# The DRAM copy of the transposed adjacency as 8-bit floats, loaded from GpSimd's queue

## The chip, the cores and the metric

The kernel runs on one core of a Trainium2 chip. The metric is the device time of one execution in microseconds. Three runs of the kernel before gave 2100.93, 2103.20 and 2105.14 us; the median is 2103.2 us. One more execution was profiled.

In the profile the engines are called PE (TensorE, matrix products), PEld (TensorE's weight loads, which overlap PE), DVE (VectorE), ACT (ScalarE), POOL (GpSimd) and SP (SyncE, which here only issues transfers). "SPq" and "POOLq" are the queues from which SP and POOL issue DMAs.

## What is computed

Two graph layers over N = 4096 nodes with 512 features. The adjacency matrix holds only zeros and ones, and is symmetric with a full diagonal. Cut to what matters (H = 8 heads, FH = 64 features a head):

```
# layer 0: graph attention with dense scores
feats   = einsum('nf,hfo->hno', x, W)
s_self  = einsum('hno,ho->hn', feats, a_self)
s_neigh = einsum('hno,ho->hn', feats, a_neigh)
dense   = s_self[:, :, None] + s_neigh[:, None, :]
dense   = where(dense > 0, dense, 0.2 * dense) * adj[None]
out     = einsum('hij,hjo->hio', softmax(dense, -1), feats) + b
x       = layernorm(x + relu(concat_heads(out)))
# layer 1: attention inside 32 graphs of 128 nodes
q, k, v = x @ Wq.T + bq, x @ Wk.T + bk, x @ Wv.T + bv
a       = where(same_graph, q @ k.T / sqrt(512), 0)
scores  = (a + adj + adj) * where(same_graph, 1, -1e6)
x       = layernorm(x + (softmax(scores, -1) * same_graph) @ v)
```

Note that a node without an edge still takes part in the softmax of layer 0, with score 0.

## The kernel before

The program holds two ways through the computation. `general_path` (line 33) is taken only for inputs that the fast one can't serve, and a flag that is computed on the chip skips it here. All the time lies in `adjacency_streamed_path` (line 405).

**Setup (to about 170 us).** Features, scores and their exponentials are computed for all nodes and put into DRAM (`g_d`, `f_d`, `pu_d`).

**Four passes, `main_pass(r)` (line 1263), two heads each.** A pass runs over 4 chunks `c` of C = 1024 target nodes, and in a chunk over 32 tiles `j` of 128 source nodes. For each (c, j) it needs `at`, a tile of A transposed: 128 source nodes in the partitions, 1024 target nodes along the row, in fp32 (512 KB). Three engines read `at`:

- VectorE makes `q` from it for each of the two heads (line 1310): the larger of `p_row` and a number of each source node, times `at`.
- ScalarE, and for one in eight VectorE, turns `q` into `mark` (lines 1319 and 1315).
- TensorE multiplies features with `at` into `accf` (line 1330), with `q` into `acc` (line 1347), and weights with `mark` into `dens` (line 1361). In pass 0 it also reads the upper half of each `at` element as bf16 (line 1374).

Work goes in cycles of `wide` tiles: 8 in passes 0 to 2, 4 in pass 3.

**Where `at` comes from: `bring` (line 1074).** In pass 0 (r = 0) GpSimd's queue loads four tiles' worth of the adjacency at once and converts it from fp32 to fp8 (`load_adjacency`, line 569, tile `a_b`); TensorE transposes it two columns at a time (line 1088), ScalarE copies the result as fp32 into `at` (line 1092), and GpSimd's queue stores it into `at_d` in DRAM (line 1093). In passes 1 to 3, `at` is loaded again from `at_d` (line 1078), by SP's queue: 3 x 128 = 384 loads. `at` has a ring of 12 buffers in passes 0 to 2 (`MORE` = 6 are added to 6) and of 6 in pass 3, so a load waits until `q`, `accf` and, in pass 0, the store have done with the tile 12 or 6 before.

**Other work on the two queues.** SP issues the loads of `f_s` and `g_s` (lines 1291 and 1295), of `p_row` and `u_row` at the start of a chunk (1269 and 1272), of `ck` (1101: the adjacency in small parts, which ScalarE checks for values other than zero and one), and in pass 3 of layer 1's inputs `x1b`, `hp_l` and `a4` (1116, 1118, 942) and the last outputs (1053). GpSimd issues, after pass 0, only the stores `hs_d` at the end of a chunk (1212) and the outputs (1053), and does small arithmetic on a few columns in pass 3: the powers of the layer norms (527 and 528) and the offsets, minima and sums of layer 1's softmax (974 to 976, 1003 to 1006, 1019 and 1020).

**Pass 3** is interleaved with layer 1: the generator `layer_1` (line 931) is advanced in pieces between the matrix products, after each chunk's rows are finished by `sums_to_rows` (line 1127) and `rows_of_layer_0` (line 1112).

**What sets the order.** The order of TensorE's instructions is that of the program text (line 455). The order on every other engine and queue is chosen at build time by a scheduler from the expected times of the instructions; each engine and queue then runs strictly in that order, and an instruction that waits holds up all that stand behind it. Waits and buffers are derived from the tiles.

Of the kernel before, what the change touches and what calls it, by code (L numbers as in the profile page):

```python
# [10 lines left out]
F32 = mybir.dt.float32  # L11
# [8 lines left out]
P = 128  # L20
# [384 lines left out]
def adjacency_streamed_path(  # L405
# [29 lines left out]
    nc = tc.nc  # L435
    N, F = x.shape
    H, _, FH = W.shape
    NT = N // P
# [5 lines left out]
    FP8 = mybir.dt.float8e4  # L444
    C = 1024
    CT = C // P
    NCH = N // C
# [12 lines left out]
    dram = ctx.enter_context(tc.tile_pool(name="fdram", bufs=1, space=DRAM))  # L460
# [1 line left out]
    g_d = dram.tile([PR, NT // 4, P, 4 * FP], F32, name="g_d")  # L462
    f_d = dram.tile([PR, NT // 4, P, 4 * 2 * FP], F32, name="f_d")
    pu_d = dram.tile([2 * H, N], F32, name="pu_d")
    at_d = dram.tile([NCH, NT, P, C], F32, name="at_d")
    hs_d = dram.tile([N, FP * (PR - 1)], F32, name="hs_d")

    ident = const.tile([P, P], F32, name="ident_f")
# [79 lines left out]
    def misc(shape, dtype=F32):  # L548

        banks.append(banks.pop(0))  # L550
        return banks[-1].tile(shape, dtype, name="ps_m")
# [4 lines left out]
    def ring(name, pool, n):  # L556

        if name not in more:
            return pool
        k = turns[name] % (n + more[name][1])  # L560
        turns[name] += 1
        return pool if k < n else more[name][0]
# [6 lines left out]
    def load_adjacency(c, j):  # L569

        a_b = pools["adj"].tile([P, CT, 4 * P], FP8, name="a_b8")
        a_bs[c, j] = a_b
        return nc.gpsimd.dma_start(
            a_b, adj[ts(c, C), j * P : (j + 4) * P].rearrange("(t p) n -> p t n", p=P)
        )


    with tc.tile_pool(name="setup1", bufs=1, side="right") as one, tc.tile_pool(
        name="setup2", bufs=2, side="right"
    ) as two, tc.tile_pool(name="setup3", bufs=3, side="right") as three, tc.tile_pool(  # L580
        name="xtp", bufs=4, side="right"
# [492 lines left out]
    def bring(r, c, j):  # L1074

        if r:
            at = ats[r, c, j] = ring("at", atp, 6).tile([P, C], F32R, name="at")
            nc.sync.dma_start(at.bitcast(F32), at_d[c, j])
            return
        if j % 2:  # L1080
            return
        if j % 4 == 0 and (c, j) not in a_bs:
            load_adjacency(c, j)
        pairs = a_bs[c, j - j % 4].rearrange("p t n -> p (t n)").bitcast(BF16)
        pairs = pairs.rearrange("p (t k n) -> p t k n", t=CT, k=2)[:, :, j % 4 // 2, :]
        pt = misc([P, CT, P], BF16)
        for t in range(CT):
            nc.tensor.transpose(pt[:, t, :], pairs[:, t, :], ident_b)
        both = pt.rearrange("p t n -> p (t n)").bitcast(FP8).rearrange("p (n k) -> p n k", k=2)
        for k in range(2):  # L1090
            at = ats[r, c, j + k] = ring("at", atp, 6).tile([P, C], F32R, name="at")
            nc.scalar.copy(at, both[:, :, k])  # L1092
            nc.gpsimd.dma_start(at_d[c, j + k], at.bitcast(F32))  # L1093
# [169 lines left out]
    def main_pass(r, ae=None, wide=4):  # L1263

        for c in range(NCH):
# [19 lines left out]
            for j0 in range(0, NT, wide):  # L1285
# [10 lines left out]
                if at_step == 0:  # L1296
                    for j in cycle:
                        bring(0, 0, j)
# [39 lines left out]
                for x_ in follow[:first]:  # L1338
                    bring(*x_)
# [41 lines left out]
                for x_ in follow[first:]:  # L1381
                    bring(*x_)
# [37 lines left out]
    with tc.tile_pool(name="lp", bufs=2) as lp, tc.tile_pool(  # L1420
        name="lp1", bufs=1
# [7 lines left out]
@with_exitstack  # L1429
def tile_gat_then_graph_attention(ctx: ExitStack, tc: tile.TileContext, *args: bass.AP):  # L1430
    nc = tc.nc
    keep = ctx.enter_context(tc.tile_pool(name="flag", bufs=1))
    flag = keep.tile([1, 1], I32, name="flag")
    adjacency_streamed_path(tc, flag, *args)
    other = nc.values_load(flag[0:1, 0:1], min_val=0, max_val=1)
    with tc.If(other > 0):
        general_path(tc, *args)
# [42 lines left out]
```

## Time and profile before

| What | Value |
|---|---|
| Runs, median | 2103.2 us (2100.93 to 2105.14) |
| Profiled execution, its own time | 2104.88 us |
| its span, first to last instruction | 2102.9 us |
| granted TensorE clock | 0.992 |
| bytes moved by DMA | 551.28 MB, mean 262 GB/s |
| HBM read and written | 491.79 MB and 107.22 MB |
| GpSimd busy | 249.4 us, 391 instructions |
| Stores `at_d`, first and last issue | 174.1 and 584.1 us |
| Loads `at`, first and last issue | 577.4 and 1941.9 us |

The span is the time between the first and the last instruction of the profiled execution; some 2 us lie around it. "Idle" of an engine is split by what ended it: an arrow `X <- Y` says that X waited and Y released it. The durations of matrix products are those of a pipeline, so a busy TensorE need not be at its peak. The DMA share is the mean busy share of 16 DMA engines; it can pass 1 where packets of two queues overlap. Bytes of a converting transfer are counted as they are written. Pass 0 runs from about 170 to 604 us, passes 1 and 2 to about 1391, pass 3 with layer 1 to about 1990, and the rest of layer 1 to the end.

### The profile page before, as it was taken

To read this page: it belongs to the slowest core of one execution; us is meant where nothing else is said; L and a number is where in the kernel's file an instruction comes from. 1 tells how busy PE (TensorE), PEld (TensorE's weight loads), DVE (VectorE), ACT (ScalarE), POOL (GpSimd) and SP (SyncE) were. 2 spreads that over 40 slices of the span, in tenths; PEclk is the share of its full clock that TensorE was granted. 3 is DMA by queue.
4 is the path that set the end of the run, shared out by engine and by line. 5 is a ranking of instruction groups with operands and counts; after the bars stand their busy time and mean duration, and the time that the engine had idled before them with its cause. 6 is when DMAs were issued, how large, how long until landed. Compare 5 with 4: busy or idle time off the path is not lost. (4 is left out here: it accounts for less than half of the span.)

```text
span 2102.9 us, 38131 instructions
## 1 busy us (share of the span) xinstructions
PE 2061.3 (98%) x15012; PEld 1015.0 (48%) x15012; DVE 1659.0 (79%) x2032; ACT 1535.7 (73%) x1818; POOL 249.4 (12%) x391
## 2 busy tenths in 40 slices
PE   8999999999999999999999999999999999999997
PEld 4545555454445544445444544444454444445443
DVE  5547788878788998787999989999975884886654
ACT  3327998888868889787899989998876666567420
POOL 2333222222100000000000000000300210210110
PEclk9999999999999999999999999999999999999999
DMA  8999999999889999887999999989964674675211
GB/s 246 270 211 243 287 285 271 294 263 278 263 286 327 338 361 344 297 301 239 323 324 343 311 327 337 334 281 362 305 238 152 239 243 144 225 270 163 73 48 42
DMA packets 207881, 551.28 MB, mean 262 GB/s; under 512 B 25292, under 2 KB 66252, under 8 KB 207692
## 3 DMA queue, kind: packets, MB, share of 16 engines
q1 hardware_dynamic: 140748, 425.79, 58.3%
q0 software_dynamic: 62784, 121.91, 23.3%
q8 instruction: 120, 1.97, 0.4%
q10 hardware_dynamic: 4160, 1.05, 0.2%
q14 instruction: 69, 0.57, 0.1%
HBM read 491.79 MB, written 107.22 MB: 285 GB/s over the span
## 5 line engine op out<-in xcount | busy, mean ns | idle before, releaser
L1310 DVE SCALAR_TENSOR_TENSOR q<-p_row,d_all,at 128x1024 f32<-128x1024 f32 x1024 | 1242.5, 1277 | 180.2 <-PE acc L1347 146.2
L1319 ACT ACTIVATE mark<-q,nb_all 128x1024 fp8e4<-128x1024 f32 x896 | 994.6, 1145 | 192.1 <-DVE q L1310 176.7
L1347 PE MATMUL acc<-q,g_s 128*32 128x512 f32 x8192 | 907.3, 594 | 3.3 <-DVE q L1310 2.9
L1347 PEld LDWEIGHTS acc<-q,g_s 128*32 128x32 f32 x8192 | 265.1, 110 | 599.2 <-issue 532.9
L1330 PE MATMUL accf<-at,f_s 128*128 128x512 f32 x2048 | 494.4, 397 | 5.5 <-DMA at<-at_d 3.9
L1330 PEld LDWEIGHTS accf<-at,f_s 128*128 128x128 f32 x2048 | 378.7, 188 | 116.0 <-issue 25.6
L1107 ACT ACTIVATE ck<-ck,neg_half_f 128x1024 f32<-128x1024 f32 x128 | 145.9, 1140 | 22.1 <-DMA ck<-in_adj_dram 22.1
L1108 ACT ACTIVATE ck<-ck,neg_quarter 128x1024 f32<-128x1024 f32 x128 | 146.3, 1143 | 1.8
L1092 ACT CAST at<-ps_m 128x1024 fp32r<-128x1024 fp8e4 x128 | 120.1, 1026 | 10.4 <-issue 5.9
L1361 PE MATMUL dens<-mark,e_b 128*6 128x512 fp8e4 x2048 | 125.0, 379 | 1.2 <-ACT mark L1319 1.2
L715 PE MATMUL ps_set<-w_sb_f,xT_f 128*128 128x512 f32 x256 | 116.4, 603 | 0.0
L957 PE MATMUL ps_m<-x1T,M_sb 128*128 128x512 f32 x256 | 113.1, 595 | 1.2 <-ACT x1T L938 1.2
L1029 PE MATMUL ps_m<-wvT,x1T 128*128 128x512 f32 x256 | 114.2, 594 | 0.0
L1212 POOL DMA_DIRECT2D hs_d<-hst x12 | 10.7, 895 | 849.6 <-DVE hst L1202 755.6
L1315 DVE TENSOR_SCALAR mark<-q,d_all 128x1024 fp8e4<-128x1024 f32 x128 | 95.7, 748 | 4.8
L737 ACT ACTIVATE fst<-fb 128x512 fp32r<-128x512 f32 x32 | 20.3, 633 | 101.5 <-DMA f_d<-fst 76.8
L1361 PEld LDWEIGHTS <-e_b 128*6 128x6 bf16 x2048 | 52.7, 86 | 81.0 <-issue 37.2
L1093 POOL DMA_DIRECT2D at_d<-at x128 | 68.7, 537 | 181.3 <-ACT at L1092 104.0
L957 PEld LDWEIGHTS ps_m<-x1T,M_sb 128*128 128x128 f32 x256 | 47.9, 190 | 62.7 <-issue 60.1
L1029 PEld LDWEIGHTS ps_m<-wvT,x1T 128*128 128x128 f32 x256 | 47.6, 190 | 57.2 <-issue 56.0
L715 PEld LDWEIGHTS ps_set<-w_sb_f,xT_f 128*128 128x128 f32 x256 | 49.1, 199 | 49.7 <-issue 49.4
L1037 DVE TENSOR_TENSOR v_t<-ps_m,bv_row 128x512 f32<-128x512 f32 x32 | 21.9, 684 | 62.2 <-PE ps_m L1029 62.2
(172 smaller groups left out, 1141.6 us busy)
## 6 DMA issues: line engine op xcount, KB each, us to landing
at<-at_d SPq DMA_DIRECT2D x384, 512.0 KB, 6.1
ck<-in_adj_dram SPq DMA_DIRECT2D x128, 512.0 KB, 5.4
f_s<-f_d SPq DMA_DIRECT2D x128, 512.0 KB, 7.6
at_d<-at POOLq DMA_DIRECT2D x128, 512.0 KB, 15.2
g_s<-g_d SPq DMA_DIRECT2D x128, 256.0 KB, 5.7
f_d<-fst POOLq DMA_DIRECT2D x32, 512.0 KB, 6.3
p_row<-pu_d SPq DMA_DIRECT2D x32, 512.0 KB, 7.1
a_b<-in_adj_dram POOLq DMA_DIRECT2D x32, 512.0 KB, 17.2
```

The costliest lines, as they stand in the source:

```text
L715: nc.tensor.matmul(pf, tile_j(xTs[k][:, c].rearrange("p u n -> p (u n)"), u), w_sb[:, c, :], start=(c == 0), stop=(c == FC - 1),)
L957: nc.tensor.matmul(pz, L1["M"][:, f, ts(c, P)], x1T[:, f, :], start=(f == 0), stop=(f == FC - 1),)
L1029: nc.tensor.matmul(pv, x1T[:, f, ts(u, P)], L1["wvT"][:, f, :], start=(f == 0), stop=(f == FC - 1),)
L1092: nc.scalar.copy(at, both[:, :, k])
L1107: tc.keep_in_program_order(nc.scalar.activation(ck, ck, AF.Square, bias=neg_half))
L1108: nc.scalar.activation(ck, ck, AF.Abs, bias=neg_quarter, accum_out=binp[:, k : k + 1])
L1310: nc.vector.scalar_tensor_tensor(q, p_row[h], d_j, ats[r, c, j].bitcast(F32), op0=OP.max, op1=OP.mult)
L1315: nc.vector.tensor_scalar(mark, q, d_j, None, op0=OP.is_gt, saturate=False)
L1319: nc.scalar.activation(mark, q, AF.Sigmoid, bias=nb_all[:, j, hh : hh + 1], scale=BIG, saturate=False,)
L1330: nc.tensor.matmul(accf[:, s, :], f_s[j // 4][:, j % 4, w, :], ats[r, c, j][:, ts(s, HB)], start=(j == 0 and w == 0), stop=(j == NT - 1 an ...
L1347: nc.tensor.matmul(acc[o : o + 32, s, :], g_s[j // 4][:, j % 4, h, o % FH : o % FH + 32], qs[j, h][:, ts(s, HB)], start=(j == 0), stop=(j ...
L1361: nc.tensor.matmul(dens[lo : lo + 6, :], e_b[:, j, 2 * r + h, :], marks[j, h][:, ts(s, HB)], start=(j == 0), stop=(j == NT - 1),)
```

## The change

```diff
@@ adjacency_streamed_path @@
-    at_d = dram.tile([NCH, NT, P, C], F32, name="at_d")
+    at_d = dram.tile([NCH, NT, P, C], FP8, name="at_d")
@@ bring @@
         if r:
             at = ats[r, c, j] = ring("at", atp, 6).tile([P, C], F32R, name="at")
-            nc.sync.dma_start(at.bitcast(F32), at_d[c, j])
+            nc.gpsimd.dma_start(at.bitcast(F32), at_d[c, j])
             return
```

The copy in DRAM holds a byte per element instead of four: 128 KB a tile, 16.8 MB in all instead of 67.1 MB. Zeros and ones are exact in it. The store of line 1093 is unchanged in the text, but now converts fp32 to fp8 on its way. The load of line 1078 converts fp8 to fp32 and is issued by GpSimd's queue instead of SP's. Tiles in SBUF, rings, cycles and all computing instructions stay as they are in the text; the scheduler places the moved loads anew.

## The prediction, made before the result was known

> **What bounds the kernel now.** I read the page's busy shares first, then the busy time by stretches, then who waited for whom, then the DMA part, and last the order of time on GpSimd's queue, because that is the queue the loads move to.
>
> ```profile
> PE 2061.3 (98%) x15012; PEld 1015.0 (48%) x15012; DVE 1659.0 (79%) x2032; ACT 1535.7 (73%) x1818; POOL 249.4 (12%) x391
> ```
>
> TensorE works 98% of the span. The stretches show where the other 42 us are (columns: engine, busy us; then clock, DMA share, GB/s):
>
> ```profile
> 260.00:700.00 440.00, 433.53 (x3888) 217.72 (x3890) 362.10 (x365) 367.66 (x362) 75.63 (x125) 1.00 1.01 283
> 700.00:1140.00 440.00, 438.95 (x3516) 214.89 (x3507) 385.06 (x367) 376.19 (x403) 3.54 (x4) 0.99 0.91 319
> 1140.00:1600.00 460.00, 456.94 (x3615) 217.27 (x3614) 410.07 (x434) 402.55 (x455) 26.16 (x21) 1.00 0.86 305
> ...
> 600.00:1000.00 400.00, 393.87 (x3134) 194.30 (x3136) 342.60 (x342) 329.63 (x352) 4.69 (x6) 0.99 0.89 313
> 1000.00:1400.00 400.00, 400.00 (x3348) 189.76 (x3344) 373.39 (x354) 359.74 (x376) 3.54 (x4) 1.00 0.92 321
> ...
> 1980.00:2103.00 123.00, 106.62 (x378) 54.59 (x370) 60.11 (x164) 21.43 (x58) 17.11 (x43) 0.97 0.17 60
> ```
>
> From 260 to 1600, where the copy is written and mostly read, TensorE idles 6.5 + 1.0 + 3.1 = 10.6 us. The rest is the setup (14 us before 260) and the tail (16 us after 1980), which hold none of the changed transfers. So even perfect loads cannot give more than about 11 us. TensorE's direct wait for the copy is smaller still (us in total, times, longest):
>
> ```profile
> PE accf L1330 <- DMA at<-at_d: 3.9, 2, 2.9
> ...
> PEld accf L1330 <- DMA at<-at_d: 7.5, 7, 3.3
> ...
> SPq L1078 <- DVE q L1310: 359.9, 192, 9.5
> ...
> POOL off L974 <- ACT a L967: 31.7, 7, 11.7
> ```
>
> Both 3.9 us waits are at the first cycle of pass 1 (608 to 616). The third line says that the loads themselves wait on SP's queue until the VectorE has released a buffer: 192 times, 1.9 us on average. The DMA part:
>
> ```profile
> at<-at_d SPq DMA_DIRECT2D x384, 512.0 KB, 6.1
> ...
> at_d<-at POOLq DMA_DIRECT2D x128, 512.0 KB, 15.2
> ...
> a_b<-in_adj_dram POOLq DMA_DIRECT2D x32, 512.0 KB, 17.2
> ```
>
> The DMA engines are 89 to 92% taken in passes 1 and 2, but nothing on TensorE's path waits for them after 616.
>
> **What the Trainium skill says.** "DMA: Bandwidth & Descriptors", section "SWDGE vs HWDGE vs iDMA": a transfer that changes type can only come from GpSimd, whose cores write each descriptor in software. The trace agrees as far as it goes: a_b, which turns fp32 into fp8, is on POOL's queue. The same page, section "Issuing engines are not separate DMA queues": whoever issues, the same 16 engines move the bytes, so I book no bandwidth for the change of queue. "SBUF — State Buffer", section "Who interferes with whom": a VectorE instruction with two SBUF inputs contends with a GpSimd instruction that reads SBUF. L1310 has two such inputs (p_row and at). The trace shows it both ways: issuing at_d took 532 to 568 ns throughout, also beside chains of L1310, and L1310 takes 1277 ns both in pass 0 (POOL issuing) and in pass 1 (POOL idle), so issuing DMAs costs neither side; but small POOL arithmetic is stretched, at worst here (order of time: start, us, what):
>
> ```profile
> 1503.69 1.17 POOL L527 TENSOR_SCALAR rstd_f<-mv_f 128x4 f32<-128x4 f32 x1 [81.11 <-DVE mv_f L525]
> ...
> 1510.27 14.02 POOL L974 TENSOR_SCALAR off<-off 128x4 f32<-128x4 f32 x1 [4.28 <-ACT a L967]
> ...
> 1507.86 8.46 DVE L1310 SCALAR_TENSOR_TENSOR q<-p_row,d_all,at 128x1024 f32<-128x1024 f32 x7
> ...
> 1516.89 6.06 DVE L1310 SCALAR_TENSOR_TENSOR q<-p_row,d_all,at 128x1024 f32<-128x1024 f32 x5
> ```
>
> An operation on 4 columns lasted 14.02 us and ended at 1524.3, just as the VectorE's chain broke off (it paused at 1524.2). I read it as shut out by that chain; a one-off cost of the operation is the other reading.
>
> **The change, part by part.**
>
> *The stores (pass 0).* 128 stores now write 128 KB instead of 512 KB. Same 128 rows, so the same 0.53 us each on POOL: 0. Transfer time: the nearest row is a_b, which also narrows fp32 to fp8. Between 464 and 466 us queue 0 moved 394 packets of 0.22 MB, nearly all a_b's (512 bytes written, 2048 read): 16 engines x 2 us / 394 = 81 ns for 512 elements. A row of 1024 elements is then 162 ns, and 8 rows per engine make 1.30 us a store. The plain rate at its fullest (0.41 MB per us at 611 to 614) gives 524 KB / 0.41 = 1.28 us. So I take the cast to run at the speed of its fp32 side: no gain, no loss, only less DRAM traffic. Pass 0 lost under 2 us outside the pass change, so a faster store would be hidden under TensorE anyway.
>
> *The loads (passes 1 to 3).* 384 loads leave SP (384 x 0.32 = 123 us of issuing) and come to POOL (384 x 0.53 = 204 us, spread over the 1365 us from 577 to 1942: 15% of POOL). POOL has room. The widening cast is shown by no row; from below it could cost its 1 KB source, about a third of now; from above twice the fp32 row, 300 ns instead of about 150 a row. I take 162 ns, the price of a_b by elements: 1.30 us a load, nothing changed. The room: 800 us of 600:1400 at a share of 0.905 leave 76 us; over 256 loads that is 0.30 us each, 37 ns a row. Up to about 190 ns a row, TensorE doesn't notice. Latency: outputs of the same 256 KB landed 2.7 us after issue from SP and 3.6 us from POOL, so +1 us. In passes 1 and 2 a load is asked for when the tile 12 before it is done; in a cycle of 8 tiles (23 to 26 us) that leaves 10 us or more beside a landing of 6.4 us. Only the hs_d stores share POOL there, one a chunk: 0.
>
> *Start of pass 1.* Loads 5 to 8 need buffers that TensorE frees at about 603. On SP they went at 604.87. On POOL they stand beside hs_d (603.32, 0.91 us) and the iota (to 604.4), then 0.6 to 0.9 us each; landing 1 us later. DMA runs at over 100% there, so I book +1 us (bounds -3.9, the whole wait, and +3).
>
> *Pass 3, GpSimd's queue.* Here POOL also does the layer norms' powers (L527, L528), the offsets (L974 to L976), L1003 to L1020 and the output stores. Every one waits for VectorE or ACT, and what stands behind it now includes the loads; and in the other direction a load that waits for a buffer now stands ahead of L527 and L528, for which the VectorE waits (24 times, at most 1.5 us). The ring is 6 tiles and a cycle 4, so a load has some 4 to 10 us in hand.
> The one place I price is 1500 to 1530: VectorE is busy 18.75 of 20 us, TensorE already waited for it (2.45 us at 1509), and loads went out at 1510.36 (two), 1515.14, 1520.31 (two) and 1523.0. Behind L974 none of them goes. VectorE then runs dry at about 1516.9, which lets L974 end; loads go from 1517 and land at about 1523.5; VectorE is 6.6 us late. TensorE's lead takes 1 to 2 of it: +5 us. Bounds: 0, if the order puts these loads ahead of L974; +12, if L974 holds the queue its full 14 us.
> For the other POOL waits of pass 3 I take +3 us: SP's queue had waits as long and TensorE lost under 1 us, but the chains POOL-VectorE-POOL are tighter. Bounds: 0, and 24 cycles x 2 us (landing 6 less 4 in hand) = 48.
>
> *SP relieved.* f_s, g_s and ck no longer stand behind loads; they wait for buffers, not for SP, and TensorE waited 0.5 us for f_s: 0.
>
> Sum: 1 + 5 + 3 = +9 us on the profiled execution's own 2104.9 us (span 2102.9), so 2113.9; that execution lies 1.7 us above the median of 2103.2, so 2112.
>
> **The rivals.**
>
> *TensorE covers all of it.* The order on POOL falls well and the one slow L974 goes unfelt: within 2 us of before, 2104. For: TensorE at 400.00 of 400 us in 1000:1400 with loads waiting in plenty. Against: 1500:1530.
>
> *Faster: the loads get a queue row of their own.* At the start of pass 1 they no longer share SP's row with u_row, f_s and g_s, and at the starts of pass 3's chunks they no longer stand behind x1b and hp_l. Gain: the 3.9 us of waits at 608 to 616 plus the 3.1 us of 1140:1600, 7 us: 2096. It decides from the point where those first loads land about 4 us sooner; against it, DMA is full there and POOL's landing is later, not sooner.
>
> *The widening cast is slow and DMA becomes the bound.* At 300 ns a row each load takes 2.4 us: 256 x 1.2 = 307 us more, less 76 of room: +231 in passes 1 and 2, about 2340; at 200 ns about +20. Against: a_b's rate.
>
> *GpSimd's queue blocks throughout pass 3.* Half to all of the 48 us: 2127 to 2151.
>
> **How the numbers follow.** A measurement here tells about 0.2%, 4.2 us, so no change is 2099.0 to 2107.4. Chances: forecast 0.50 (own range 2107 to 2125), covered 0.27, faster 0.08, queue blocks throughout 0.08, slow cast 0.07. Slower is 0.50 + 0.08 + 0.07 = 0.65. The range 2099 to 2145 leaves out the faster case, the slow cast and a third of the blocking queue, 0.18.
>
> **What would show it.** Right: at<-at_d on POOLq, landing near 7 us; DMA share in 700:1140 still about 0.9; TensorE idle in 600:1400 hardly changed, and a new idle of some us near 1510 to 1530 put down to DMA or to VectorE waiting for at, with a POOL operation ahead of late loads. Wrong: a DMA share at 1.0 with TensorE waiting in passes 1 and 2 (slow cast); no new wait in pass 3 (covered); a first cycle of pass 1 without its 3.9 us (faster).

## The result, and the profile after

Four runs of the changed kernel gave 2122.46 to 2131.52 us, median 2126.94, against a median of 2103.8 us for the kernel before, run beside it. The ratio is 1.0112, 95% interval 1.0093 to 1.0131: slower by 23 us. The profiled execution took 2131.52 us (span 2129.3, granted clock 0.987), which is the slowest of the four; its span is 26.4 us longer than that of before. Which part of this belongs to the change is worked out below.

First the page of the kernel after: busy shares, a group of instructions, HBM traffic, and the DMA issues (KB each, median us from issue to landing).

```profile
PE 2074.4 (97%) x15012; PEld 1020.0 (48%) x15012; DVE 1659.7 (78%) x2032; ACT 1538.1 (72%) x1818; POOL 444.7 (21%) x775
...
L1078 POOL DMA_DIRECT2D at<-at_d x384 | 208.6, 544 | 952.2 <-DVE q L1310 491.5
...
HBM read 340.79 MB, written 56.89 MB: 187 GB/s over the span
...
at<-at_d POOLq DMA_DIRECT2D x384, 512.0 KB, 5.1
at_d<-at POOLq DMA_DIRECT2D x128, 128.0 KB, 14.8
a_b<-in_adj_dram POOLq DMA_DIRECT2D x32, 512.0 KB, 16.0
```

The change does what it says. The 384 loads are on GpSimd's queue at 0.54 us each, HBM moves 201 MB less, and the converting loads land 1.0 us sooner than the plain ones did (5.1 against 6.1 us). VectorE and ScalarE have the work that they had. TensorE's busy time, however, has grown by 13.1 us for the same 15012 products, and its idle time by the other 13.3.

Who waited for whom, first before, then after (us in total, times, longest):

```profile
PE acc L1347 <- DVE q L1310: 2.9, 3, 2.5
```

```profile
PE acc L1347 <- DVE q L1310: 13.3, 6, 5.0
PE accf L1330 <- DMA at<-at_d: 4.9, 2, 4.0
...
POOL off L974 <- ACT a L967: 21.1, 5, 7.7
```

The wait for `at` has grown little (3.9 before). What is new is that TensorE waits for `q`, VectorE's product. Three stretches, before and then after, show where (window; its length; busy us of PE, PEld, DVE, ACT, POOL; clock, DMA share, GB/s):

```profile
560.00:650.00 90.00, 84.92 (x731) 39.54 (x732) 75.03 (x87) 63.88 (x62) 5.39 (x10) 1.00 0.78 283
650.00:1380.00 730.00, 728.95 (x5930) 353.50 (x5926) 654.55 (x626) 638.95 (x677) 7.11 (x8) 1.00 0.91 321
1380.00:1500.00 120.00, 120.00 (x992) 55.38 (x984) 113.02 (x119) 107.98 (x115) 0.89 (x1) 1.00 0.91 324
```

```profile
560.00:650.00 90.00, 82.02 (x653) 38.00 (x653) 65.18 (x73) 57.58 (x58) 18.51 (x35) 0.94 1.03 248
650.00:1380.00 730.00, 729.18 (x5935) 353.94 (x5937) 652.72 (x630) 637.75 (x675) 133.52 (x247) 1.00 1.00 316
1380.00:1500.00 120.00, 111.24 (x872) 50.31 (x868) 98.94 (x98) 97.52 (x117) 19.46 (x34) 0.96 0.92 300
```

In the 730 us of passes 1 and 2 nothing has changed for TensorE. The losses lie in the first cycle of pass 1 and in the first chunk of pass 3; in both, the clock column falls below 1.00.

TensorE in order of time (start, us, what; in brackets the idle time before it and who ended it), before:

```profile
602.51 1.08 PE L1374 MATMUL ae<-at,e_p 128*25 128x512 bf16 x16
604.32 3.90 PE L1330 MATMUL accf<-at,f_s 128*128 128x512 f32 x16 [0.73 <-PE ae L1374]
611.09 3.77 PE L1330 MATMUL accf<-at,f_s 128*128 128x512 f32 x12 [2.87 <-DMA at<-at_d]
...
617.00 13.94 PE L1347 MATMUL acc<-q,g_s 128*32 128x512 f32 x128
630.76 1.91 PE L1361 MATMUL dens<-mark,e_b 128*6 128x512 fp8e4 x32
```

and after:

```profile
607.61 1.08 PE L1374 MATMUL ae<-at,e_p 128*25 128x512 bf16 x16
609.41 3.92 PE L1330 MATMUL accf<-at,f_s 128*128 128x512 f32 x16 [0.73 <-PE ae L1374]
617.35 3.92 PE L1330 MATMUL accf<-at,f_s 128*128 128x512 f32 x8 [4.02 <-DMA at<-at_d]
...
625.90 7.52 PE L1347 MATMUL acc<-q,g_s 128*32 128x512 f32 x64
635.16 9.85 PE L1347 MATMUL acc<-q,g_s 128*32 128x512 f32 x62 [1.75 <-DVE q L1310]
644.43 0.60 PE L1361 MATMUL dens<-mark,e_b 128*6 128x512 fp8e4 x4
...
1417.61 4.75 PE L1347 MATMUL acc<-q,g_s 128*32 128x512 f32 x16 [3.65 <-DVE q L1310]
...
1450.35 4.83 PE L1347 MATMUL acc<-q,g_s 128*32 128x512 f32 x16 [4.96 <-DVE q L1310]
```

Take the rows as marks. The end of pass 0 is 5.1 us late already (602.51 to 607.61). 4.3 us of it are there before the change can act: the first store of the copy is issued at 178.4 us against 174.1. The rest lies within the spread: over the thirteen profiled kernels of this study (one execution each) the first row above starts at times from 600.0 to 607.7, and among the late ones is a kernel whose stores and queue are those of before (6.3 below, 606.35). The first cycle then takes 8.6 us longer (630.76 less 602.51 against 644.43 less 607.61): 1.2 us in the wait for `at`; 2.6 us from there to the first `acc` (8.55 against 5.91), although the products are the same; and 4.8 us in `acc` (18.53 against 13.76), of which 1.75 is a wait and most of the rest is that 62 products take 9.85 us where 128 took 13.94. The two rows of pass 3 stand for 3.65 and 4.96 us of waiting, and each of the 16-product rows that follow takes some 3 us longer than 16 products of a 128-row do (13.94 / 8 = 1.74): 6.7 and 8.0 us. 5.1 + 8.6 + 6.7 + 8.0 = 28.4, against 26.4 of the span; some of it is recovered.

Why VectorE is late is in its own order of time, after:

```profile
629.93 0.43 DVE L921 COPY kb<-b_k 128x512 f32<-128x512 f32 x1 [13.51 <-DMA b_k<-in_L_gnn_bk_dram]
...
1415.81 0.56 DVE L1123 SCALAR_TENSOR_TENSOR x1b<-hp_l,x1b 128x384 f32<-128x384 f32 x1 [4.48 <-DMA hp_l<-hs_d]
...
1447.35 0.56 DVE L1123 SCALAR_TENSOR_TENSOR x1b<-hp_l,x1b 128x384 f32<-128x384 f32 x1 [6.79 <-DMA hp_l<-hs_d]
```

A copy that prepares layer 1 stands in front of the `q` of the first cycle and waits 13.5 us for a bias of 2 KB. Two additions of layer 1 stand in front of the `q` of pass 3 and wait for `hp_l`. Before, the same copy ran at 712.98 without a wait. SP's queue tells what moved, before:

```profile
689.81 1.48 SPq L876 DMA_DIRECT2D b_k<-in_L_gnn_bk_dram  x1
...
722.82 0.43 SPq L884 DMA_DIRECT2D w_q<-in_L_gnn_Wq_dram  x1
```

and after:

```profile
611.79 0.65 SPq L876 DMA_DIRECT2D b_k<-in_L_gnn_bk_dram  x1
612.49 1.58 SPq L884 DMA_DIRECT2D w_q<-in_L_gnn_Wq_dram  x1
...
615.82 0.85 SPq L884 DMA_DIRECT2D w_k<-in_L_gnn_Wk_dram  x1
```

Layer 1's loads had stood behind the `at` loads on SP's queue. With those gone the scheduler issues them 78 to 110 us earlier, in the fullest DMA window of the kernel, and it moves the VectorE instructions that use them forward with them. Issued at 611.79, the 2 KB bias (512 elements of 4 bytes) took 18.0 us to land.

Where the products slow down, the stretches of TensorE show this (columns: window, its length, busy us of TensorE, clock, DMA share, GB/s):

```profile
612.00:616.00 4.00, 1.33 (x6) 1.00 1.31 285
616.00:620.00 4.00, 2.65 (x6) 0.58 1.41 281
620.00:624.00 4.00, 3.08 (x7) 0.50 2.02 344
624.00:628.00 4.00, 4.00 (x21) 0.64 1.90 378
628.00:632.00 4.00, 4.00 (x44) 1.00 1.22 395
...
1452.00:1456.00 4.00, 4.00 (x16) 0.50 0.72 218
```

After the wait of 4.02 us the clock falls to a half, and again after the one of 4.96 us. The first three stretches below 1.00 lack (0.42 + 0.50 + 0.36) x 4 = 5.1 us of full clock; at half rate that is some 10 us, an estimate. The Trainium skill ("TensorE: Matmul & The Clock Gate", Part 1, on the HAM clock gate) says that after an idle window of about 3.4 us TensorE runs at half rate until it has been busy for about as long, and that the window runs free of the program. The waits of 4.02 and 4.96 us agree, and so does the one of 2.87 us at the same place before, which left the clock at 1.00. As a sharp threshold it does not hold here: before's wait of 2.45 us at 1509 was followed by a stretch at 0.72. How long the half rate lasts is not measured apart here, since TensorE waited again for 0.92 us in between.

### The profile page after: what moved, and what is told of

Read it like the earlier page. It is cut to its first block, busy times and chain, and to the rows that moved or that the text cites. A ratio compares the mean times of both kernels' runs of the same rounds, so it can differ in the third digit from the quotient of the medians.

```text
span 2129.3 us, 38141 instructions
## 1 busy us (share of the span) xinstructions
PE 2074.4 (97%) x15012; PEld 1020.0 (48%) x15012; DVE 1659.7 (78%) x2032; ACT 1538.1 (72%) x1818; POOL 444.7 (21%) x775
## 5 line engine op out<-in xcount | busy, mean ns | idle before, releaser
L1347 PE MATMUL acc<-q,g_s 128*32 128x512 f32 x8192 | 913.7, 595 | 14.7 <-DVE q L1310 13.3
L1078 POOL DMA_DIRECT2D at<-at_d x384 | 208.6, 544 | 952.2 <-DVE q L1310 491.5
## 6 DMA issues: line engine op xcount, KB each, us to landing
at_d<-at POOLq DMA_DIRECT2D x128, 128.0 KB, 14.8
```

The costliest lines, as they stand in the source:

```text
L1078: nc.gpsimd.dma_start(at.bitcast(F32), at_d[c, j])
L1347: nc.tensor.matmul(acc[o : o + 32, s, :], g_s[j // 4][:, j % 4, h, o % FH : o % FH + 32], qs[j, h][:, ts(s, HB)], start=(j == 0), stop=(j ...
```

## The experiments

Three theories were put against each other. A: the emptied SP queue lets the scheduler pull layer 1's loads and their users forward. B: the loads are held up on GpSimd's queue by what stands there (the prediction's steps). C: the converting transfer itself costs time. Ratios are to the kernel before, run beside each batch.

**1. The queue alone.** The copy in DRAM stays fp32; the order on TensorE, VectorE, ScalarE and SP is that of the kernel after, instruction by instruction. (On GpSimd's queue one `a_b` load and one `at` load change places with stores of pass 0.)

```diff
-    at_d = dram.tile([NCH, NT, P, C], FP8, name="at_d")
+    at_d = dram.tile([NCH, NT, P, C], F32, name="at_d")
```

> The copy stays fp32 in DRAM; only the queue of the loads changes. VectorE, ScalarE, SP and TensorE have the same order of instructions as in the changed kernel. Theory A (emptying SP's queue let the scheduler bring other loads and the VectorE work on them forward): as slow as the changed kernel, 2120 to 2130. Theory B (loads are held up on GpSimd's queue by what stands ahead of them): the same, 2120 to 2130. Theory C (the converting transfers cost the time): back to 2101 to 2107.

Measured: 2131.29 us, ratio 1.0126 (1.0110 to 1.0142). As slow as the full change without any conversion in `at_d`: C falls. VectorE waits at the same copy as long as in the kernel after. The row names an `at` load, but the copy reads `b_k` alone, which landed at 624.51:

```profile
624.63 0.43 DVE L921 COPY kb<-b_k 128x512 f32<-128x512 f32 x1 [13.59 <-DMA at<-at_d]
```

**2. Layer 1's loads alone.** The kernel before, fp32, `at` loads on SP. Now the others leave: the loads of lines 876, 884, 1116 and 1118 go to GpSimd's queue.

```diff
-            nc.sync.dma_start(ws[name], w.rearrange("(c p) f -> p c f", p=P))
+            nc.gpsimd.dma_start(ws[name], w.rearrange("(c p) f -> p c f", p=P))
...
-            nc.sync.dma_start(x1b[:, u, :], x[ts(it, P), :])
+            nc.gpsimd.dma_start(x1b[:, u, :], x[ts(it, P), :])
...
-            nc.sync.dma_start(hp, hs_d[ts(it, P), :])
+            nc.gpsimd.dma_start(hp, hs_d[ts(it, P), :])
```

> The kernel before (copy in fp32, its loads on SP, no conversion), with the loads of layer 1's biases, weights and inputs (lines 876, 884, 1116, 1118) moved to GpSimd's queue, which is free there. VectorE's order becomes that of the changed kernel at the start of pass 1 and in pass 3's first chunk. Theory A: nearly as slow as the changed kernel, 2115 to 2132, with VectorE waiting for b_k and hp_l. Theory B (the copy's loads are held up on GpSimd's queue) and theory C (conversion): no reason for a loss, 2101 to 2108.

Measured: 2125.78 us, ratio 1.0097 (1.0081 to 1.0112). Nothing of the change is in this kernel, neither the 8-bit copy nor an `at` load on GpSimd's queue; what it shares with it is that layer 1's loads no longer queue behind `at`. The loss is nearly the same. The profiled execution (2118.99 us) was the fastest of the four and so shows less than the median does, but in the same two places: from the end of pass 0 to the second cycle's `accf` it takes 39.5 us (39.5 in the kernel after, 30.1 before), and in the 120 us from 1380 TensorE idles 5.9 us (8.8 after, none before). The three weights, 1 MB each, are issued at 604.6 to 606.1 us, and TensorE's row after the first 16 `accf` and a row in pass 3 read:

```profile
612.43 2.08 PE L1330 MATMUL accf<-at,f_s 128*128 128x512 f32 x4 [5.32 <-DMA at<-at_d]
...
1436.87 3.11 PE L1347 MATMUL acc<-q,g_s 128*32 128x512 f32 x16 [2.67 <-DVE q L1310]
```

Here TensorE waits longer for `at` (9.1 us in four waits at the start of pass 1, against 4.9 in two), with the three weights in flight beside it, and VectorE hardly for the copy (0.19 us): the same bias, issued from GpSimd's queue at 603.87, landed in 5.7 us. That the mechanism is the same holds for the early loads, not for each wait.

**3. Holding single instructions (three kernels).** In the kernel after, the weight loads of line 884 keep their place in the program text:

```diff
-            nc.sync.dma_start(ws[name], w.rearrange("(c p) f -> p c f", p=P))
+            tc.keep_in_program_order(
+                nc.sync.dma_start(ws[name], w.rearrange("(c p) f -> p c f", p=P)))
```

> The changed kernel, with the three 1 MB weight loads of layer 1 kept in program order on SP, so that they come 80 us and more after the start of pass 1 again; the copy kb still stands early on VectorE. Theory A: the start of pass 1 regains part of its 8.6 us, 3 to 8: 2118 to 2124; landing of the first loads of pass 1 falls from 12.5 us. Theories B and C: unchanged, 2122 to 2131.

Measured: 2125.41 us, ratio 1.0094 (1.0080 to 1.0108), not told apart from the kernel after. `w_q` went back to 738 us, but `b_k` is still issued at 607.8, and the copy still waits 13.78 us: the weights are not what makes the 2 KB late. Next, the additions of line 1123 that read `hp_l`, in program order:

```diff
-                nc.vector.scalar_tensor_tensor(dst, src, 0.0, dst, op0=OP.max, op1=OP.add)
+                (tc.keep_in_program_order if src is hp else id)(
+                    nc.vector.scalar_tensor_tensor(dst, src, 0.0, dst, op0=OP.max, op1=OP.add))
```

> The changed kernel, with the four additions of hp_l (line 1123) kept in program order on VectorE. Theory A: the two stalls of TensorE in the first chunk of pass 3 (3.65 and 4.96 us) go, with the slower matrix products after them, 12.9 us in all; some is given back at the ends of the chunks: 2112 to 2120. Theory B: unchanged, since GpSimd's queue and what stands ahead of the loads is nearly the same, 2122 to 2131. Theory C: unchanged.

Measured: 2127.69 us, ratio 1.0115 (1.0098 to 1.0132): no gain, a miss for A's number. The stalls on `hp_l` at 1416 and 1447 went, and another took their place, on ScalarE, first row, with TensorE behind it, second row:

```profile
1425.69 0.31 ACT L967 ACTIVATE a<-a 128x128 f32<-128x128 f32 x1 [7.75 <-DMA a<-in_adj_dram]
...
1427.76 0.60 PE L1361 MATMUL dens<-mark,e_b 128*6 128x512 fp8e4 x4 [7.21 <-ACT mark L1319]
```

`a4` is one more load of layer 1 that came forward, and its first user is pulled in front of ScalarE's `mark`. The held additions also cost something where they now stand, at the end of the chunk: VectorE waits 4.0 us for `hp_l` there, and TensorE 4.9 and 2.4 us for `q` (1523 and 1527). Both holds together:

> Both of the former together. Theory A: the sum, 2104 to 2114. Theories B and C: unchanged, 2122 to 2131.

Measured: 2128.93 us, ratio 1.0112 (1.0093 to 1.0132); the stall stays with ScalarE (7.5 us in `dens`, in two waits). These are misses for A's numbers. They narrow the theory: to hold one instruction wasn't enough, since the user of another early load came to stand in the way.

**4. The copy left out.** `kb` is not made; TensorE reads the bias through a broadcast view.

```diff
-        nc.vector.tensor_copy(kb, cols["k"][:, :, None].to_broadcast([P, FC, P]))
+        kb = cols["k"][:, :, None].to_broadcast([P, FC, P])
```

> The changed kernel without the VectorE copy kb (line 921): TensorE takes the broadcast view of b_k itself, so nothing on VectorE waits for b_k. Theory A: VectorE's 13.5 us wait at the start of pass 1 goes, TensorE gains its 1.7 to 3.7 us wait and the 3 us of slower products after it: 4 to 7 us under the changed kernel, 2118 to 2124. Theory B: unchanged, 2122 to 2131.

Measured: 2123.81 us, ratio 1.0085 (1.0071 to 1.0099). VectorE's wait for `b_k` at the start of pass 1 is gone, but TensorE waits at the next mark, for `f_s`, which is issued among the early weights (its wait goes in 6.1, where they are held):

```profile
644.11 5.35 PE L1330 MATMUL accf<-at,f_s 128*128 128x512 f32 x16 [4.01 <-DMA f_s<-f_d]
```

**5. Pass 3 mended.** In the kernel after, the additions of `hp_l` in line 1123 are tied to the last `q` of a cycle, one a cycle, and line 967 keeps its place in the text. (The lines that remember each `q` in `qi` are not shown here.)

```diff
+    spaced = lambda it, ins: tc.add_manual_dep(
+        ins.ins, qi[PR - 1, it // CT, 4 * (it % CT) + 3].ins.name,
+        mybir.DependencyInfo(mybir.DependencyClass.NoSync, mybir.DependencyReason.DATA),
+        reason="spaced")
...
-                nc.vector.scalar_tensor_tensor(dst, src, 0.0, dst, op0=OP.max, op1=OP.add)
+                spaced(it, nc.vector.scalar_tensor_tensor(dst, src, 0.0, dst, op0=OP.max, op1=OP.add))
...
-                    nc.scalar.activation(
+                    tc.keep_in_program_order(nc.scalar.activation(
```

> The changed kernel with one addition of hp_l allowed per cycle of pass 3 (each stands behind the last q of its own cycle) and ScalarE's scaling of a4 (line 967) in program order. The loads stay on GpSimd's queue and are converted. Theory A: the stalls of pass 3's first chunk go without new ones: 10 to 13 us under the changed kernel, 2112 to 2119. Theory B: unchanged, 2122 to 2131.

Measured: 2111.64 us, ratio 1.0025 (1.0017 to 1.0033). The first chunk of pass 3 is whole again:

```profile
1380.00:1500.00 120.00, 120.00 (x1012) 54.61 (x1006) 113.80 (x117) 105.87 (x114) 19.44 (x36) 1.00 1.05 339
```

Of the 1.1% some three quarters are won back without touching the queue or the 8-bit copy. The holds of this kernel and the missing copy together:

> no_kb and spaced_a4 together. Theory A: nearly the kernel before, 2104 to 2112; what stays above it is GpSimd's own share. Theory B: at most half of the loss comes back, 2115 or more.

Measured: 2111.45 us, ratio 1.0032 (1.0020 to 1.0044): no further gain, as `f_s` is still late (3.6 us at 643.4).

**6. All four holds, and two controls.** 6.1: fix of 5, no copy, and the weights of 3 in program order.

> The kernel after with all four holds: the add of line 1123 held to one a cycle, ScalarE's line 967 in program order, no copy kb, and the weight loads of line 884 in program order, so that f_s of the first cycle of pass 1 no longer stands behind them. Theory A (what was pulled forward costs the time): the 3.6 to 4 us wait for f_s at the start of pass 1 goes and with it some 4 to 7 us; 2102 to 2109. Theory B (loads held up on GpSimd's queue): as with three holds, 2109 to 2114.

Measured: 2109.31 us, ratio 1.0009 (1.0000 to 1.0018): of the 1.1% about a tenth is left, and TensorE's wait for `f_s` is gone. But the start of pass 1 is not mended: from the end of pass 0 to the second cycle's `accf` it still takes 37.7 us (30.1 before, 39.5 after). With the copy and the weights held, yet another early load has taken their place. `p_if` (line 824), the 33 numbers that bound layer 1's graphs, is issued at 612.6 us (849.6 before), and VectorE waits for it in front of `q`:

```profile
628.25 0.15 DVE L826 CAST p_ff<-p_if 33x1 f32<-33x1 int32 x1 [11.72 <-DMA p_if<-in_L_gnn_ptr_dram]
```

So the total is near that of before although these 7.6 us are still lost; by the next run it is the conversion that makes up for them. 6.2: the same with `at_d` in fp32. The order is the same on every engine and on SP's queue; on GpSimd's the two loads named in 1 change places again.

> The four holds on the kernel after with the DRAM copy left fp32; every engine and queue has the same order as with the 8-bit copy, so the conversion is the only difference. If the conversion costs or gains nothing also where no other stall covers it: within 3 us of the kernel with four holds. If the fewer bytes in DRAM bring the loads in sooner at the start of pass 1, where TensorE waits 4 us for at: 3 to 5 us slower than it. If the conversion is dearer than it looked: faster than it by 3 us or more.

Measured: 2118.36 us, ratio 1.0049 (1.0033 to 1.0066): 9 us slower than with the 8-bit copy. So the conversion doesn't cost; here it gains, and by more than was expected. The DMA part, first of the 8-bit kernel, then of this one:

```profile
at<-at_d POOLq DMA_DIRECT2D x384, 512.0 KB, 5.2
```

```profile
at<-at_d POOLq DMA_DIRECT2D x384, 512.0 KB, 6.7
```

The loads land 1.5 us sooner. From the end of pass 0 to the first chunk's rows in pass 3 (line 1201 at 605.0 and 1429.0, against 603.7 and 1433.4) the 8-bit kernel is 5.7 us shorter, and after that another 3.3 us. Which single waits make up these 9 us was not taken further, so why the conversion gains is not shown. 6.3: the same four holds on the kernel before.

> Control: the same four holds on the kernel before, fp32 copy and loads on SP's queue. If the holds only undo what the change pulled forward, the kernel before gains nothing from them: 2100 to 2107. If they are a gain of their own, which the change merely shares, it is faster than before by as much as the kernel after gained, some 15 us: 2085 to 2095.

Measured: 2106.73 us, ratio 1.0001 (0.9990 to 1.0012). The holds are no gain of their own: what they win back on the changed kernel is what it had lost. Pass 0 of this kernel ended late as well (the same row at 606.35), though its stores and loads are those of before. No kernel tried was faster than the one before.

## Why the prediction was right or wrong

The direction was right and the size too small: +23 us on the medians against a forecast of +9. The time, 2126.94 us, lies inside the wide range of 2099 to 2145, but outside the 2107 to 2125 that was given to the forecast's own mechanism. That mechanism, waits on GpSimd's queue, is not the one that acted, so the right direction and the hit of the range are luck as far as the cause goes.

- **The stores, 0.** Right. TensorE was busy 387.2 us of 170 to 560, 386.8 before, and the store lands in 14.8 us (15.2).
- **The loads, 1.30 us each, passes 1 and 2 unchanged.** Right in its effect: 729.18 busy of 730 us against 728.95. The added latency of 1 us did not come: plain fp32 loads from GpSimd's queue landed in 6.2 us (1), those from SP's in 6.1, and the converting ones in 5.1. The sign that was to show a slow cast, a DMA share of 1.0, came (1.00 in 650 to 1380) with TensorE idle for 0.8 of 730 us: the share of these converting loads is no measure of how much room is left.
- **Start of pass 1, +1 (bounds -3.9 and +3).** Mis-sized: +8.6, outside its bounds. The wait for `at` did grow by 1.2 us, as priced. What had no term was VectorE's copy waiting for `b_k`, and the clock, which fell to a half after the wait of 4.02 us where it had stayed at 1.00 after 2.87.
- **Pass 3, L974, +5.** Fell. The 14 us row did not come back: L974's longest in the kernel after is 1.3 us, and at most 1.8 us in every other kernel run here, the old queue in 6.3 among them. The other reading that the prediction gave, a one-off, is the one that the runs support. That L974's wait would hold loads back did not decide either, as it shrank (31.7 to 21.1 us).
- **Other waits on GpSimd's queue, +3.** Not seen. The new waits of pass 3 are for `hp_l` and, once that is held, for `a4`. Neither is on GpSimd's queue.
- **SP relieved, 0.** This is the step that failed. It reasoned that the loads left on SP "wait for buffers, not for SP". That named only f_s, g_s and ck, and left out `b_k`, the weights, `p_if`, `x1b`, `hp_l` and `a4`: what kept these late was the queue, and that was useful, since it kept their users out of VectorE's and ScalarE's way and some of the loads out of the fullest DMA window. Experiment 2 shows nearly the whole loss without any part of the change itself, and 6.1 takes about nine tenths of it away with the change left in. A part of that is the conversion's own gain, which stands against a loss that the holds leave. With fp32 in both, so that the conversion plays no part, the four holds bring the move of queue from 1.0126 to 1.0049: some six tenths of that loss are the order that they mend.
- **Two readings beside the sum.** The idle before 260 us was said to hold none of the changed transfers; the stores begin at 174.1, but only 1.8 of those 14 us lie after 170. And the slow cast's sum takes 1.2 us more a load, where its 2.4 less the 1.30 booked are 1.1. Nothing rests on either.

Of the rivals, the one with the queue blocked throughout pass 3 named 2127 as its lower end, and that is the time measured, again by luck and not by its mechanism: the new waits of pass 3 are on VectorE and ScalarE, and they go when those engines' orders are held (5) with the loads left on GpSimd's queue. The slow cast is excluded by 1 and 6.2. The faster one named a gain from separate queue rows, and no run shows one: in 1 the fp32 loads have left SP's queue, and TensorE waits 4.1 us for them at the start of pass 1, where it was 2.9 before. The conversion's gain of 9 us (6.1 against 6.2) is something else, since the queue is the same in both; it only makes up for what the move alone still loses with the four holds (1.0049).

Open: the remaining 0.5% of 6.2. Its profile puts the loss at the start of pass 1: from the end of pass 0 to the second cycle's `accf` it takes 9.9 us longer than before, to the end of the span 9.7 us longer. VectorE waits 14.0 us there in front of the cast that reads `p_if`, TensorE 4.2 us for `at` and 2.6 us for `q`. That is theory A once more, with a load that no hold touched, but no run holds `p_if` as well, so it is argued and not shown. Theory B, the loads being held up on GpSimd's queue, may have a part in the wait for `at`. Whether the conversion gains as much in the unmended order was not settled either: 1.0112 against 1.0126, with intervals that overlap.

## What to carry to other kernels

When transfers leave a queue, list what stood behind them: a scheduler will move these loads up, and with them the instructions of in-order engines that use them. Price where they land and what waits behind their first user, not only the transfers that were moved. When one such instruction is held, look at what the scheduler puts in its place: here `a4` and `p_if` followed on `hp_l` and `b_k`. A wait of some 4 us on TensorE cost more than its length here, since the clock fell after it (4.02 and 4.96 us), so it is worth asking what could lengthen a wait of 3 us.

## What had not been expected of the hardware

- Waits of TensorE were followed by a half clock: 3.51 us in 6.3 by 0.50 in the 4 us from 616, 4.02 us in the kernel after by 0.58, 0.50 and 0.64. In the kernel after, the 16 `accf` products behind that wait and the way to the first `acc` took 8.55 us against 5.91, so the wait cost some 2.6 us on top of its length (the pauses between the products are in that figure). Shorter waits did it in some places and not in others: 2.87 us left 1.00, 2.64 us in 6.2 was followed by 0.71.
- TensorE that has caught up with VectorE shows as busy. 62 `acc` products in 9.85 us are 159 ns each, 8 of them 1271 ns: the duration of one `q` (1279 ns median), which feeds 8 products. The clock was 1.00 in most of that row. Busy time that grows with the same count of instructions is thus two things here, a lower clock and the pace of a feeding engine; that the pace is VectorE's is read from the match of the two times, not tested.
- A transfer of 2 KB in elements of 4 bytes, issued on SP's queue when DMA was full, took 18.0 us to land, longer than the 512 KB loads of the same stretch (12.5 us median). Without the weights beside it, it took 18.3 us (3); from GpSimd's queue, ahead of the weights, 5.7 us at a DMA share of 0.90 (2). So a full DMA alone does not account for it; what does was not tested.
- A load that widens 8-bit to fp32 landed 1.0 to 1.5 us sooner than the plain fp32 load of the same size in SBUF from the same queue (5.1 against 6.2 us in 1, 5.2 against 6.7 in 6), and cost GpSimd no more to issue (544 against 542 ns).
